# An attention block over 16 images: first image opened in a pinned order, and two inner sums of the third head issued earlier

## The chip, the cores and the metric

The kernel runs on one core of one Trainium2 chip. The metric is device time in microseconds. Five runs of the kernel before lie between 3180.75 and 3183.3, with a median of 3181.74. The profile is one further execution.

In the profile, PE is TensorE's matmul and PEld its weight load, DVE is VectorE, ACT is ScalarE, POOL is GpSimd and SP is SyncE. A letter q behind an engine's name (SPq, ACTq, POOLq) is its sequencer, where transfers are issued. L12 is line 12 of the kernel.

## The reference

For each of 16 images of 512 channels and 32 x 32 = 1024 positions, all in float32:

```python
xg = x.reshape(b, NUM_GROUPS, -1)                       # 8 groups of 64 channels
xn = ((xg - mu) * rsqrt(var + EPS)).reshape(b, c, h, w) * gamma + beta
qkv = einsum('oc,bchw->bohw', qkv_w, xn) + qkv_b        # 1536 x 512
attn = softmax(einsum('bhnd,bhmd->bhnm', q, k) * dh ** -0.5)   # 4 heads of 128
out = einsum('bhnm,bhmd->bhnd', attn, v)
return x + einsum('oc,bchw->bohw', proj_w, out) + proj_b
```

## The kernel before

**Tiles.** An image is four chunks of 128 channels by 1024 positions. Chunks 0 and 1 are the upper rows of the block matrix b (blocks b11 and b12, the left and the right half of the positions), chunks 2 and 3 the lower ones (b21, b22). A float32 matmul shows as two rows in the profile.

**Products by sevens.** The projections for q and k (two pairs of heads), for v and at the end use Strassen's method in Winograd's form: seven products of blocks, with sums of blocks in front and sums of results behind. `FACTORS` names the two factors of each product: 1 is (a11, b11), 2 is (a12, b21), 3 is (s4, b22), 4 is (a22, t4), 5 is (s1, t1), 6 is (s2, t2), 7 is (s3, t3). The weights give s1 = a21 + a22, s2 = s1 - a11, s3 = a11 - a21, s4 = a12 - s2. The images give t1 = b12 - b11, which is written over b12, t2 = b22 - t1, t3 = t2 - b11, t4 = b21 - t2. So b11 and t1 need the upper chunks alone, and t2, t3 and t4 need all. Products go in the `ORDER` 1, 2, 6, 5, 7, 4, 3. `strassen` (L448) holds the accumulation: 1, 6, 7 and 4 share the PSUM bank `x`, 5 and 3 share a bank `y`, and 2 has a `y` bank of its own. The pool has two banks with the tag `y`, and the small products `pm` and `pv` of the group norm use the same tag. The scores use the tag `s` in another pool.

`two_levels` (L514) applies the method twice: four outer groups of at most two products each, and seven inner products in each group. `make_sum` (L526) makes the inner sums t1 to t4 of a group on DVE (L537). For an image's first pair of heads, from image 1 on, they are also kept in DRAM by a transfer on POOL's queue (L541, `sums="keep"`), from where the v products read them. Results of group g are collected in a tile `r` with the tag g % 3, so group 0 of the next products shares its tile with group 3 of the last ones. `v_units` (L680), used for image 0 alone, has one level.

**Image 0.** Its loads are halves of chunks, on the SP and the ACT queue. Constants (gamma, beta and the biases) follow on ACT's queue (L231). `stage_v` and `stage_blocks` put weights on SP's queue. Sixteen matmuls of a constant matrix (`warm`, L1088) keep PE busy while the chunks arrive. `Norm` holds the group norm's steps: `chunk` makes the statistics of a chunk on DVE; `group` averages over channels with a first small matmul (`pm`, L53), makes the variance and averages again (`pv`, L64), then `ve`, a power on POOL (`rstd`, L68) and `sc`; `shift` makes `t` and `sh`; `apply` normalises half a chunk on ACT (L86) or DVE (L89). In image 0 the upper and the lower chunks are two separate groups of statistics. Even chunks are normalised on DVE and odd ones on ACT. For later images ACT makes the statistics from sums and sums of squares (L244 to L250), during the attention of the image ahead.

**Attention.** The main loop runs over heads and eight blocks of 128 keys: scores (L798), exponential on ACT (L804), sum of the exponentials into `tot` on DVE (L810, L812), weighted sum (`po`, L894). `plan_head` deals other work into the eight blocks. During an image's head 1 (the second) these are the projection of the image ahead of it, and the statistics, the normalising and t1 of the next image. During head 2 (the third) it is the q and k products of the next image's first pair. The projection's `finish` adds bias, residual and results to a tile `y` (L778, L781) and stores it with a transfer on POOL's queue (L782).

**What sets the order.** The framework's scheduler takes traced instructions by priority and by the times that its cost model gives, engine by engine; on the chip each engine then runs its list in order. `tc.high_priority(URGENT)` raises the priority of what is traced inside it. `tc.issue_after(ins)` puts what is traced inside behind `ins` on that instruction's engine, in order of issue only. `tc.keep_in_program_order(ins)` puts `ins` behind the last instruction traced on its engine. Before the change only some of DVE's work in image 0 is held by `issue_after`, behind `ve` of the lower rows or behind a normalising.

Of the kernel before, what the change touches and what calls it, by code (L numbers as in the profile page):

```python
# [16 lines left out]
P = 128  # L17
# [13 lines left out]
class Norm:  # L31


    def __init__(self, nc, gn, ps, avg, neghalf, gamma, beta, ncc, n, tag="acc"):
        self.tag = tag
        self.nc, self.gn, self.ps, self.avg, self.neghalf = nc, gn, ps, avg, neghalf
        self.gamma, self.beta, self.ncc, self.n = gamma, beta, ncc, n

    def chunk(self, mv, x, c):
        nc = self.nc  # L40
        st = self.gn.tile([P, self.n // HALF, 6], F32, tag="st", name="st")
        for h in range(self.n // HALF):
            nc.vector.bn_stats(st[:, h, :], x[:, ts(h, HALF)])
        nc.vector.bn_aggr(mv[:, c, :], st.rearrange("p h s -> p (h s)"))

    def group(self, mv, first=0):


        nc, gn, k = self.nc, self.gn, mv.shape[1]
        mean = gn.tile([P, k], F32, tag="mean", name="mean")  # L50
        nc.vector.tensor_copy(mean, mv[:, :, 0])
        pm = self.ps.tile([P, HALF], F32, tag=self.tag, name="pm")
        nc.tensor.matmul(pm[:, :k], self.avg, mean, start=True, stop=True)  # L53

        d = gn.tile([P, k], F32, tag="d", name="d")
        nc.vector.tensor_sub(d, mean, pm[:, :k])
        d2 = gn.tile([P, k], F32, tag="d2", name="d2")
        nc.vector.tensor_mul(d2, d, d)
        v = gn.tile([P, k], F32, tag="vv", name="vv")
        nc.vector.tensor_add(v, d2, mv[:, :, 1])  # L60
        mu = gn.tile([P, k], F32, tag="mu", name="mu")
        nc.vector.tensor_copy(mu, pm[:, :k])
        pv = self.ps.tile([P, HALF], F32, tag=self.tag, name="pv")
        nc.tensor.matmul(pv[:, :k], self.avg, v, start=True, stop=True)  # L64
        ve = gn.tile([P, k], F32, tag="ve", name="ve")
        self.last = nc.vector.tensor_scalar_add(ve, pv[:, :k], EPS)
        rstd = gn.tile([P, k], F32, tag="rstd", name="rstd")
        nc.gpsimd.tensor_tensor(rstd, ve, self.neghalf[:, :k], ALU.pow)  # L68
        sc = gn.tile([P, k], F32, tag="sc", name="sc")
        nc.vector.tensor_mul(sc, rstd, self.gamma[:, first : first + k])  # L70
        return mu, sc

    def shift(self, mu, sc, first=0):

        nc, k = self.nc, mu.shape[1]
        t = self.gn.tile([P, k], F32, tag="t", name="t")
        nc.vector.tensor_mul(t, mu, sc)
        sh = self.gn.tile([P, k], F32, tag="sh", name="sh")
        nc.vector.tensor_sub(sh, self.beta[:, first : first + k], t)
        return sh  # L80
# [76 lines left out]
KC = 2  # L157
# [6 lines left out]
def fast_path(ctx, tc, x, sources, out, consts, flag, dims):  # L164
# [63 lines left out]
    for t, src in (  # L228
        (gamma_sb, gamma), (beta_sb, beta), (qkb_sb, qk_b), (vb_sb, v_b), (projb_sb, proj_b)
    ):  # L230
        nc.scalar.dma_start(t, src)  # L231

    norm = Norm(nc, gn, ps_a, avg, neghalf, gamma_sb, beta_sb, NCC, N, "y")

    def stats_chunk(b, c):
        if c == 0:
            mvs[b] = gn.tile([P, NCC, 2], F32, tag="mv", name=f"mv_{b}")
        if b == 0:
            norm.chunk(mvs[b], xs[b, c], c)
            return  # L240

        junk = lpool.tile([P, N], F32, tag="tt", name=f"junk_{b}_{c}")
        sums = gn.tile([P, 3], F32, tag="st", name=f"sums_{b}_{c}")
        nc.scalar.activation(junk, xs[b, c], AF.Identity, accum_out=sums[:, 0:1])  # L244
        nc.scalar.mul(mvs[b][:, c, 0:1], sums[:, 0:1], 1.0 / N)
        nc.scalar.mul(sums[:, 1:2], sums[:, 0:1], -1.0 / N)
        nc.scalar.activation(
            junk, xs[b, c], AF.Square, bias=sums[:, 1:2], accum_out=sums[:, 2:3]
        )
        nc.scalar.mul(mvs[b][:, c, 1:2], sums[:, 2:3], 1.0 / N)  # L250

    def stats_group(b, first=0, last=NCC):
        mu, sc = norm.group(mvs[b][:, first:last, :], first)
        sh = norm.shift(mu, sc, first)
        for c in range(first, last):
            scaled[b, c] = sc, sh, c - first

    def normalise(b, c, half):
        t = xs[b, c][:, ts(half, HALF)]
        sc, sh, i = scaled[b, c]  # L260

        return norm.apply(t, t, sc, sh, i, b > 0 or c % 2 == 1)

# [156 lines left out]
    def stage_v():  # L420
# [8 lines left out]
        base = 2 * C  # L429
        for n in ("a11", "a12", "a21", "a22"):  # L430
            r, kk = int(n[1]) - 1, int(n[2]) - 1
            for k in range(KC):
                nc.sync.dma_start(
                    wv[n][:, k, :], qkv_wT[ts(KC * kk + k, P), ds(base + r * HC, HC)]
                )

    def v_sums():
        nc.vector.tensor_sub(wv["s3"], wv["a11"], wv["a21"])
        nc.vector.tensor_sub(wv["s4"], wv["a12"], wv["s2"])

# [3 lines left out]
    def run(units):  # L444
        for u in units:
            u()

    def strassen(name, mm, out_, width=HALF):  # L448

# [18 lines left out]
        def p2():  # L468
            t["y"] = bank("y")
            mm(t["y"], 2, True)  # L470
            out_("c11", t["y"], t["p1"])

# [21 lines left out]
        units = {1: p1, 2: p2, 3: p3, 4: p4, 5: p5, 6: p6, 7: p7}  # L494
        return [units[i] for i in ORDER]

    def two_levels(name, site, b, blocks, finish, sums="make", homes="BBBB", prepare=None):
# [31 lines left out]
        def make_sum(g, m):  # L529
# [5 lines left out]
            }[m]  # L535
            for i in range(n):
                nc.vector.tensor_sub(to[:, i, :], inner_block(g, i, a), inner_block(g, i, c))  # L537
            if sums == "keep":
# [137 lines left out]
    def v_units(b, jj):  # L676
# [28 lines left out]

        return strassen(f"v_{b}_{jj}", mm, out_)

# [380 lines left out]
    def warm(n, name):  # L1088

        acc = ps_s.tile([P, HALF], F32, tag="s", name=name)  # L1090
        for _ in range(n):
            ins = nc.tensor.matmul(acc[:, :P], avg, avg, start=True, stop=True)
            tc.keep_in_program_order(ins)

    stage_v()
    stage_blocks(0)
    warm(16, "warm")

    for c in range(KC):
        stats_chunk(0, c)  # L1100
    with tc.high_priority(URGENT):
        stats_group(0, 0, KC)
        for half in range(NH2):
            for c in range(KC):
                upper = normalise(0, c, half)
    for c in range(KC, NCC):
        stats_chunk(0, c)
    stats_group(0, KC, NCC)
    before_power = norm.last
    for half in range(NH2):  # L1110
        for c in range(KC, NCC):
            ins = normalise(0, c, half)
            last_normal = ins if c % 2 == 0 else last_normal
    with tc.issue_after(before_power.ins):
        nc.vector.tensor_add(wv["s1"], wv["a21"], wv["a22"])
        nc.vector.tensor_sub(wv["s2"], wv["s1"], wv["a11"])
        x_sums(0, (1,))
    with tc.issue_after(last_normal.ins):
        sums_of_b(xb[0], (2, 3))
        v_sums()  # L1120
    run(staggered([v_units(0, 0), v_units(0, 1)], (0, 1)))
    stage_sums(0)
    run(staggered(qk_groups(0, 0)))
    next_v, next_qk = [], [qk_groups(0, 1)]
# [168 lines left out]
```

## Time and profile before

| | |
|---|---|
| median of 5 runs | 3181.74 us (3180.75 to 3183.3) |
| the profiled execution | 3181.31 us |
| its span on the core | 3179.5 us |
| PE busy | 3163.6 us, 99% of the span |
| DVE busy | 2630.4 us, 83% |
| ACT busy | 1441.7 us, 45% |
| POOL busy | 514.8 us, 16% |
| matmuls of the scores and of the weighted sum | 1047.1 and 1048.9 us |
| first v matmul of image 0 | at 13.78 us |
| first q and k matmul of image 0 | at 39.91 us |

The span is the time from the first to the last instruction on the core. A group of rows in a timeline gives start, length, engine, line, operation, output and inputs, and the count; in square brackets stands the idle time of the engine ahead of it and what ended that. Matmuls overlap in the pipeline, and their ends are modelled: where a few tenths matter, the starts of successive rows are compared.

### The profile page before, as it was taken

Reading aid. Unit: us, or ns where it says so; the run is one execution under the profiler, and the core shown is the slowest. Engines: PE = TensorE matmul, PEld = TensorE weight load, DVE = VectorE, ACT = ScalarE, POOL = GpSimd, SP = SyncE. Lnnn points to the kernel's source line nnn. Section 1 sums busy time; section 2 is a strip of 40 time slices with the busy share of each in tenths; the row PEclk is TensorE's granted clock in tenths of the full one; section 3 lists DMA queues with packets and bytes.
Section 4 is the critical chain, followed back from the end, with each engine's and each line's share of the span. In section 5 each row is a group of like instructions: output and inputs, shape, how many; then the busy total and the mean of one; then the engine's idle time right before and its main releaser. Section 6 shows DMA issues by size and latency. Waiting matters only on the chain.

```text
span 3179.5 us, 34082 instructions
## 1 busy us (share of the span) xinstructions
PE 3163.6 (99%) x10496; PEld 2187.6 (69%) x10496; DVE 2630.4 (83%) x4634; ACT 1441.7 (45%) x2709; POOL 514.8 (16%) x893
## 2 busy tenths in 40 slices
PE   9999999999999999999999999999999999999999
PEld 7566676676766766677666677667676676766764
DVE  8878979788897888878888787987879978788784
ACT  2535435354353543535435454453534545344342
POOL 0011221111211112211122111222012221122200
PEclk9999999999999999999999999999999999999999
DMA  5655554545545555454554545555455553555531
GB/s 169 214 185 158 183 177 148 176 151 193 166 158 162 163 182 176 163 168 145 191 173 159 175 140 188 167 173 175 138 179 170 176 183 132 181 160 184 181 126 41
DMA packets 211308, 526.92 MB, mean 166 GB/s; under 512 B 32816, under 2 KB 65840, under 8 KB 211120
## 3 DMA queue, kind: packets, MB, share of 16 engines
q1 hardware_dynamic: 133312, 284.74, 28.7%
q0 software_dynamic: 63840, 204.53, 18.9%
q10 hardware_dynamic: 13968, 35.41, 3.5%
q8 instruction: 86, 1.41, 0.2%
q14 instruction: 102, 0.84, 0.1%
HBM read 389.56 MB, written 135.00 MB: 165 GB/s over the span
## 4 chain that ended last, share of the span: by engine, by line
PE 87%; DVE 10%; issue 2%; POOL 1%; DMA 1%; SPq 0%; ACT 0%; ACTq 0%; POOLq 0%; DVEq 0%
PE po L894 24%; PE s L798 24%; PE qk_x L567 12%; PE qk_y L567 9%; PE v_x L567 6%; PE v_y L567 4%; PE pp_x L567 4%; PE pp_y L567 3%; DVE y L781 2%; DVE tot L812 2%; DVE y L778 2%; DVE pp_r L587 1%; DVE pp_r L634 1%; POOL rstd L68 1%; DVE o L904 1%
## 5 line engine op out<-in xcount | busy, mean ns | idle before, releaser
L894 PE MATMUL po<-p,v 128*128 128x512 f32 x2048 | 1048.9, 594 | 0.0
L798 PE MATMUL s<-qk,qk 128*128 128x512 f32 x2048 | 1047.1, 593 | 1.3 <-ACT p L804 1.3
L804 ACT ACTIVATE p<-s 128x512 f32<-128x512 f32 x1024 | 610.6, 597 | 932.8 <-PE s L798 931.6
L894 PEld LDWEIGHTS po<-p,v 128*128 128x128 f32 x2048 | 602.8, 302 | 316.9 <-issue 212.1
L812 DVE TENSOR_TENSOR tot<-tot,p 128x1024 f32<-128x1024 f32 x385 | 470.0, 1221 | 161.6 <-ACT p L804 161.6
L798 PEld LDWEIGHTS s<-qk,qk 128*128 128x128 f32 x2048 | 387.6, 190 | 89.1 <-issue 28.0
L567 PEld LDWEIGHTS qk_x<-qk_t,w 128*128 128x128 f32 x1344 | 250.4, 190 | 171.6 <-issue 76.4
L567 PE MATMUL qk_x<-qk_t,w 128*128 128x256 f32 x1344 | 357.3, 382 | 1.1 <-ACT qk_u L461 1.1
L461 ACT COPY qk_u<-qk_x 128x512 f32<-128x512 f32 (+1 forms) x256 | 136.3, 533 | 230.9 <-PE qk_x L567 226.1
L731 POOL DMA_DIRECT2D vd<-vu x120 | 66.6, 557 | 909.6 <-DVE vu L723 902.3
L587 DVE TENSOR_TENSOR qk_r<-qk_y,qk_u 128x512 f32<-128x512 f32 (+1 forms) x256 | 158.6, 620 | 36.5 <-ACT qk_u L461 22.4
L567 PE MATMUL pp_x<-pp_t,w_proj 128*128 128x256 f32 x630 | 169.3, 385 | 0.0
L782 POOL DMA_DIRECT2D out_y<-y x120 | 66.0, 550 | 632.7 <-DVE y L781 630.5
L587 DVE TENSOR_TENSOR v_r<-v_y,v_u 128x512 f32<-128x512 f32 (+1 forms) x120 | 76.2, 635 | 110.5 <-ACT v_u L461 80.3
L736 POOL DMA_DIRECT2D v<-vd x240 | 140.5, 592 | 162.5 <-DMA vd<-vu 78.5
L567 PE MATMUL v_x<-v_t,w_v 128*128 128x256 f32 x630 | 166.6, 381 | 0.0
L541 POOL DMA_DIRECT2D kept_t<-qk_t x240 | 129.2, 540 | 223.5 <-DVE qk_t L537 204.0
L567 PEld LDWEIGHTS pp_x<-pp_t,w_proj 128*128 128x128 f32 x630 | 116.1, 190 | 64.2 <-issue 22.2
L567 PEld LDWEIGHTS v_x<-v_t,w_v 128*128 128x128 f32 x630 | 118.4, 190 | 55.3 <-issue 19.1
L567 PE MATMUL qk_y<-x,w 128*128 128x256 f32 x512 | 141.8, 379 | 0.0
L666 DVE SCALAR_TENSOR_TENSOR qk<-qk_r,qkb_sb,qk_r 128x512 f32<-128x512 f32 x192 | 137.8, 745 | 1.6
L461 ACT COPY v_u<-v_x 128x512 f32<-128x512 f32 (+1 forms) x124 | 66.3, 535 | 156.8 <-PE v_x L567 130.3
(204 smaller groups left out, 4491.9 us busy)
## 6 DMA issues: line engine op xcount, KB each, us to landing
kept_t<-qk_t POOLq DMA_DIRECT2D x180, 256.0 KB, 3.1
w<-kept SPq DMA_DIRECT2D x90, 512.0 KB, 4.0
v_t<-kept_t SPq DMA_DIRECT2D x180, 256.0 KB, 2.9
w<-kept SPq DMA_DIRECT2D x90, 384.0 KB, 3.4
rinv<-row ACTq DMA_DIRECT2D x63, 512.0 KB, 4.8
x<-in_x POOLq DMA_DIRECT2D x60, 512.0 KB, 5.1
vd<-vu POOLq DMA_DIRECT2D x120, 256.0 KB, 3.0
v<-vd POOLq DMA_DIRECT2D x240, 128.0 KB, 4.2
```

Source lines behind the costliest of these rows:

```text
L461: nc.scalar.copy(t[n][:, :width], t["x"][:, :width])
L541: nc.gpsimd.dma_start(t, to)
L567: nc.tensor.matmul(acc[:, ts(i, Q)], have["w"][t][:, i, slot, :], inner(i, bn), start=(first and i == 0), stop=True, skip_group_check=True,)
L587: nc.vector.tensor_add(dst, view(a), view(c))
L666: nc.vector.scalar_tensor_tensor(st[b, h][:, ts(half, HALF)], a, qkb_sb[:, i : i + 1], c, ALU.add, ALU.add)
L731: nc.gpsimd.dma_start(rows[which][ts(h, P), :], u)
L736: nc.gpsimd.dma_start(vs[b, pair][ts(q, BLK), half].rearrange("m h (k i) j -> m (h k) (i j)", k=n), rows[which].rearrange("(k m) (q e) -> ...
L782: nc.gpsimd.dma_start(out[b, ts(o, P), ts(half, HALF)], t)
L798: nc.tensor.matmul(sc, ks[b, h][:, ts(j, P)], qs[b, h][:, ts(half, HALF)], start=True, stop=True)
L804: exps[s] = nc.scalar.activation(ps[s][:, ts(half, HALF)], sc, AF.Exp, scale=SCALE)
L812: added[b, h, j] = nc.vector.tensor_add(tot[b, h][:, i], tot[b, h][:, i], ps[s][:, i])
L894: nc.tensor.matmul(po[b, h][:, i], v_block(b, h, j), ps[s][:, i], start=(j == 0), stop=(j == NB - 1),)
```

## The change

It has two parts.

The first is `open_image`, which replaces the opening of image 0. Most of its instructions on DVE, and the upper rows' on PE, are pinned to their order in the program. The `Norm` methods are cut into lists of steps for this (`chunk_steps`, `group_steps`), with the same instructions. Twenty warm matmuls stand ahead of `pm`, two between `pm` and `pv`, eight behind `pv`. Chunk 3's statistics are made on ACT. The upper rows' left halves are both normalised on DVE and their right halves on ACT; the lower rows stay as before. v's products are run in the order 1, 5, 2, 6, 7, 4, 3, both units abreast, and product 2 has a bank with the tag `s`. The constants are loaded on POOL's queue. v's weights arrive in the order a11, a21, a22, a12. All DVE work of the v units and of the first pair's q and k products comes behind the last t2.

The second is in `make_sum`: from image 1 on, t1 and t2 of group 0 of the first pair are issued behind the last addition to `tot` of the head ahead, with raised priority.

```diff
-        nc.scalar.dma_start(t, src)
+        nc.gpsimd.dma_start(t, src)
...
-        for n in ("a11", "a12", "a21", "a22"):
+        for n in ("a11", "a21", "a22", "a12"):
...
         def p2():
-            t["y"] = bank("y")
-            mm(t["y"], 2, True)
-            out_("c11", t["y"], t["p1"])
+            own = upper_first
+            acc = ps_s.tile([P, HALF], F32, tag="s", name=f"{name}_z") if own else bank("y")
+            mm(acc, 2, True)
+            out_("c11", acc, t["p1"])
...
-        return [units[i] for i in ORDER]
+        return [units[i] for i in ((1, 5, 2, 6, 7, 4, 3) if upper_first else ORDER)]
...
-            for i in range(n):
-                nc.vector.tensor_sub(to[:, i, :], inner_block(g, i, a), inner_block(g, i, c))
+            with ExitStack() as order:
+                if sums == "keep" and g == 0 and m in ("t1", "t2"):
+                    order.enter_context(tc.issue_after(added[b - 1, 1, NB - 1].ins))
+                    order.enter_context(tc.high_priority(URGENT))
+                for i in range(n):
+                    nc.vector.tensor_sub(
+                        to[:, i, :], inner_block(g, i, a), inner_block(g, i, c)
+                    )
...
+    def open_image():
+        pin = tc.keep_in_program_order
+        norm.pin = pin
...
+        warm(20, "warm_0")
+        for c in range(KC):
+            steps(norm.chunk_steps(mvs[0], xs[0, c], c), 0, 1, 2)
+        with tc.high_priority(URGENT):
+            g = norm.group_steps(mvs[0][:, upper, :])
+            steps(g[:2], 0, 1)
+            warm(2, "warm_1")
+            steps(g[2:8], 0, 1, 2, 3, 4, 5)
+            warm(8, "warm_2")
+
+        stats_chunk(0, NCC - 1)
+        third = norm.chunk_steps(mvs[0], xs[0, KC], KC)
+        steps(third[:1], 0)
+        steps(g[8:], 0, 1)
+        shift(g, upper)
+        for half in range(NH2):
+            for c in range(KC):
+                pin(normalise(0, c, half, half == 1))
+        steps(third[1:], 0, 1)
+        with tc.high_priority(URGENT):
+            g = norm.group_steps(mvs[0][:, lower, :], KC)
+            steps(g[:2], 0)
+            sum_(wv["s1"], wv["a21"], wv["a22"], True)
+            steps(g[2:7], 0, 1, 2, 3)
+        xb[0] = halves([xs[0, c] for c in range(NCC)], "x")
+        bl = xb[0]
+        sum_(bl["t1"][0], bl["b12"][0], bl["b11"][0])
+        with tc.high_priority(URGENT):
+            steps(g[7:9], 0, 1)
+        sum_(bl["t1"][1], bl["b12"][1], bl["b11"][1])
+        with tc.high_priority(URGENT):
+            steps(g[9:], 0)
+        shift(g, lower)
+        for half in range(NH2):
+            for c in range(KC, NCC):
+                pin(normalise(0, c, half, c % 2 == 1))
+        norm.pin = lambda ins: ins
+        sum_(wv["s2"], wv["s1"], wv["a11"])
+        for k in range(KC):
+            last = sum_(bl["t2"][k], bl["b22"][k], bl["t1"][k])
+        with tc.issue_after(last.ins):
+            for k in range(KC):
+                nc.vector.tensor_sub(bl["t3"][k], bl["t2"][k], bl["b11"][k])
+            nc.vector.tensor_sub(wv["s3"], wv["a11"], wv["a21"])
+            for k in range(KC):
+                nc.vector.tensor_sub(bl["t4"][k], bl["b21"][k], bl["t2"][k])
+            nc.vector.tensor_sub(wv["s4"], wv["a12"], wv["s2"])
+        return last
...
-    warm(16, "warm")
...
-    run(staggered([v_units(0, 0), v_units(0, 1)], (0, 1)))
-    stage_sums(0)
-    run(staggered(qk_groups(0, 0)))
+    opened = open_image()
+    with tc.issue_after(opened.ins):
+        run(staggered([v_units(0, 0), v_units(0, 1)], (0, 0)))
+        stage_sums(0)
+        run(staggered(qk_groups(0, 0)))
```

## The prediction

> **What bounds the kernel now.** First the page's table of busy times and PE's own waits.
>
> ```profile
> PE 3163.6 (99%) x10496; PEld 2187.6 (69%) x10496; DVE 2630.4 (83%) x4634; ACT 1441.7 (45%) x2709; POOL 514.8 (16%) x893
> ...
> PE pv L64 <- DVE vv L60: 2.5, 2, 1.3
> PE qk_y L567 <- DVE qk_t L537: 2.2, 14, 0.2
> PE warm L1092 <- DVE avg L225: 1.5, 1, 1.5
> PE pm L53 <- DVE mean L51: 1.3, 1, 1.3
> ```
>
> PE is the bound: a change can win only where PE waits or runs slowly. The waits of any size are in the opening (warm, pm, pv), plus one small wait that comes back 14 times. The clock column of the stretches shows what waits alone don't (columns: busy us of PE, PEld, DVE, ACT, POOL, then the granted clock):
>
> ```profile
> 9.00:10.00 1.00, 0.38 (x2) 0.30 (x2) 1.00 (x5) 0.00 (x0) 0.00 (x0) 1.00 0.48 134
> 10.00:11.00 1.00, 0.03 (x1) 0.04 (x1) 1.00 (x6) 0.00 (x0) 0.00 (x0) 0.87 0.74 169
> 16.00:17.00 1.00, 1.00 (x4) 0.75 (x3) 1.00 (x5) 0.00 (x0) 0.00 (x0) 0.50 0.72 194
> 18.00:19.00 1.00, 1.00 (x7) 0.87 (x6) 1.00 (x4) 1.00 (x3) 0.00 (x0) 1.00 0.90 266
> 20.00:60.00 40.00, 40.00 (x184) 34.03 (x184) 38.81 (x92) 10.91 (x20) 0.00 (x0) 1.00 0.43 143
> ```
>
> The clock falls to 0.50 after PE had little to do, and v's first products pay for it. The last line matters later: DVE is nearly full behind a full PE. Third, the timeline of the opening:
>
> ```profile
> 7.63 0.69 DVE L43 BATCH_NORM_STATS2 st<-x 128x6 f32<-128x512 f32 x1 [0.60 <-DMA x<-in_x]
> 9.39 0.38 PE L53 MATMUL pm<-mean,avg 128*128 128x2 f32 x2 [1.30 <-DVE mean L51]
> 10.97 0.59 PE L64 MATMUL pv<-vv,avg 128*128 128x2 f32 x2 [1.20 <-DVE vv L60]
> 13.78 5.57 PE L684 MATMUL v_x<-wv_a,x 128*128 128x256 f32 x16
> 31.27 3.62 PE L684 MATMUL v_x<-wv_a,xt 128*128 128x256 f32 x16
> ```
>
> The first 16 v matmuls take 5.57 us, sixteen of the same kind 3.62 once the clock is full. Last, the start of a third head (image 5's; the others look alike):
>
> ```profile
> 1128.16 1.22 DVE L812 TENSOR_TENSOR tot<-tot,p 128x1024 f32<-128x1024 f32 x1
> 1129.29 0.69 DVE L781 TENSOR_TENSOR y<-y,pp_r 128x512 f32<-128x512 f32 x1
> 1129.89 0.75 DVE L778 SCALAR_TENSOR_TENSOR y<-pp_r,projb_sb,y 128x512 f32<-128x512 f32 x1
> 1130.56 0.43 DVE L537 TENSOR_TENSOR qk_t<-x 128x256 f32<-128x256 f32 x1
> 1130.89 0.69 DVE L781 TENSOR_TENSOR y<-y,pp_r 128x512 f32<-128x512 f32 x1
> 1131.22 0.59 PE L567 MATMUL qk_y<-qk_t,w 128*128 128x256 f32 x2
> 1131.49 0.43 DVE L537 TENSOR_TENSOR qk_t<-x 128x256 f32<-128x256 f32 x1
> 1131.98 0.70 PE L567 MATMUL qk_y<-qk_t,w 128*128 128x256 f32 x2 [0.16 <-DVE qk_t L537]
> 1132.51 1.02 PE L798 MATMUL s<-qk,qk 128*128 128x512 f32 x2
> ```
>
> The second t1 sum waits behind the projection's last additions, and PE waits for it. The row says 0.16 because ends are modelled; read the starts. A row of this form occupies PE for 0.216 (sixteen in 3.62, of which the last shows 0.38), a pair for 0.43. Here the next start comes 0.76 after the first pair and 0.53 after the second: 0.33 and 0.10, together 0.43 lost.
>
> **Third head's first sums.** Four inner sums of group 0 (t1 and t2, two each) go directly behind `tot`'s eighth addition. Nothing is added, but DVE's order changes: they start at 0.33 spacing (1130.56 to 1130.89) from 1129.3, and the last is done by 1130.7, ahead of the wait at 1131.65. Their inputs are there: the outer t1 (L283) ends by 1127.9. Gain 14 x 0.43 = 6.0 us. The trace's fifteenth third head (image 0) starts on another wait, so I count 14; 15 would be 6.5. What moves back is y's three additions, by 4 x 0.33 = 1.3 us. They feed only POOL's output DMAs, with nothing on PE behind them. Behind them stands qk's first c11 addition (1131.83), which writes the result tile that the projection's last group still occupies: 0.7 us later (1129.3 + 1.3 + 1.97 for the three = 1132.57). It releases a `y` bank; next taken by qk at 1141.20, 8.7 us on. t2's DMA to the kept sums goes out on POOL earlier, before the last output DMAs instead of after (1131.88, 1132.41); each is 0.54 of a POOL busy 16%.
>
> **The opening up to v.** DVE's aggregate of chunk 1 stood behind a chunk 2 half that waited 0.60 for its transfer; pinned in order, the mean is ready by 7.4. But PE now runs 20 warm matmuls first: sixteen (32 rows) took 6.60, four more take 0.9 at full rate (0.113 a row, half of 3.62/16) or 1.65 at the average. pm thus starts at 8.9 to 9.7 against 9.39; I take 8.9, as the tail is the fast part. From there by rows: pm to d 0.45, three small DVE steps 0.17 each, pv to ve 0.62, ve to the power 0.25, power to sc 0.75, sc to the first normalise 0.59, that to the first v matmul 0.60: 12.6 instead of 13.78. Gain 1.2 (0.3 at the other end). The warm matmuls between pm, pv and v (2 and 8) fill gaps of 1.30 and 1.20 (0.45 and 1.8 us at 0.113 a row), leaving about 0.4 and 0.6. With that I expect the clock to hold: 5.57 - 3.62 = 1.95 more. The other end is nothing, if it falls again.
> [...]
>
> **The lower rows inside v.** The second pm and pv now run between v's products: 133.09 to 133.34 and 135.27 to 135.51 in a later image, so 0.5 us. The new product order (1, 5, 2, ...) puts lower rows third. By 3.62 a pair of products, v 1 starts at 12.6, 5 at 16.7, 2 at 20.3, 6 at 23.9, 7 at 27.5. DVE, in pinned order: two normalises to 13.0, statistics 0.64 + 0.19, mean, s1 0.68 while pm runs, four small steps to 15.2, t1 0.69, ve, t1 by 16.6, power 1.08, sc and shift to 17.6, normalise to 18.7, s2 and t2 to 20.6, t3, s3, t4, s4 to 24.5. Only t1 is close (16.6 against a second step at 17.1). ACT takes chunk 3's statistics: 1.05 + 1.14 and four reads and scalings of 0.19 from the landing at 9.3 (its bn_stats started 9.24) gives 12.5, then 2 x 0.8 to 14.1, in front of t1. Bounds 0 to 1.5 lost here.
>
> **Costed at nothing.** Constants go from ACT's queue to POOL's: five of 0.55 each from 0.8, landing within 5.1 (the x rows of POOL), so by 8.7, when gamma is wanted at 11.5. If that cover went, sc would wait and v with it, microsecond for microsecond.
> [...]
> v's weights in order a11, a21, a22, a12 are the same eight transfers. p2's own bank comes from the scores' pair, free until 65. DVE behind the opening: s4 ends at 24.5 instead of 23.34 while PE is 2.65 ahead, so DVE is 3.8 us tighter. Cover: qk's third group of weights ends at 41.35 (L413 at 40.93) and its first product runs at 50.64; the first group's has over 10 us. If it is not enough, up to 2.65 goes.
>
> **Sum.** 6.0 + 1.2 + 1.95 - 0.5 = 8.65. The profiled execution took 3181.31 (span 3179.5): 3172.7. The median 3181.74 stands 0.43 higher: 3173.1.
>
> **Rivals.** 0.2% is 6.4 us, about what a measurement here can tell from no change.
> A, the opening gives nothing (clock falls again, or PE waits at t1, pm or for DVE's backlog): 3181.7 - 6.0 = 3175.7, up to 3177 with a microsecond of new waits. For it: DVE's 38.81 of 40. Against: the slack above.
> B, the change doesn't do what it says: the third head's sums do not help, because another addition is late in their place (the c11 addition, t3 at 1133.1): 3181.7 - 2.65 = 3179.1. Against: DVE's total in that stretch is unchanged, and p6 at 1133.37 and what follows had its sums in time.
> C, slower: the c11 addition, 0.7 late, holds the bank or result tile that PE's next group wants, in 15 images: 15 x 0.74 = 11.1 - 2.65 gives 3190.2. It decides from 0.19 us an image (2.65/15), by more than the measure from 0.6. Against: 8.7 us of slack on the bank. An order made anew by the planner could shrink it.
> D, better: fifteen heads at 0.43, pm as soon as the mean is there (7.4, another 1.5), small matmuls hidden: 3170.5 or less.
>
> **How the numbers follow.** Forecast (3170.5 to 3175.3) 0.60, A 0.15, B 0.09, C 0.09, D 0.07. Faster: forecast and D, 0.67. Same: A and B, 0.24. Slower: C, 0.09. The range leaves out C and the far part of D: 3169.5 to 3179.5; the forecast's own is 3170.5 to 3175.3.
>
> **What would show it.** Right: no line of PE qk_y waiting for qk_t 14 times; pairs of qk_y starting 0.43 apart; four L537 rows in a row behind L812; granted clock 1.00 from 10 on; v's first 16 rows in about 3.6 from 12.6; qk's first product near 37.2 instead of 39.91. Wrong: a clock of 0.50 in 10 to 18, v_x waiting for wv_s or x sums, or a new PE wait repeated by image.

## The result, and the profile after

The changed kernel takes 3174.48 us (median of 25 runs, 3173.08 to 3176.53) against 3181.68 us (45 runs, 3179.92 to 3183.3). The ratio is 0.9978, with a 95% interval of 0.9973 to 0.9984: 7.2 us less. The interval lies clear of 1, but it reaches across 0.998, so the change is faster by about the 0.2% that the prediction took as what can be told from no change. The profiled execution took 3174.56 us, its span is 3172.8 us.

The total is near the forecast of 3173.1, but not for the reasons given. The third heads brought more than forecast, and the opening brought almost nothing to the end. The page's busy times first.

```profile
PE 3159.3 (100%) x10524; PEld 2197.8 (69%) x10524; DVE 2629.7 (83%) x4631; ACT 1443.4 (45%) x2716; POOL 515.6 (16%) x898
```

PE is busy for 4.3 us less (3163.6 before), although it runs 28 rows more, the warm matmuls. Busy time counts a slow clock and modelled ends too, so it is not a count of work. PE's own waits in the changed kernel (total us, times, longest) are more telling:

```profile
PE qk_x L592 <- ACT qk_r L610: 1.9, 1, 1.9
PE warm L1117 <- DVE avg L248: 1.5, 1, 1.5
...
PE pm L83 <- DVE mean L82: 1.2, 1, 1.2
PE qk_x L592 <- DMA w<-kept: 0.8, 1, 0.8
```

The wait of `qk_y` for `qk_t`, 14 times, is gone, and so are the waits for `vv` (2.5) and the early `pm` (1.3). Two large ones are new: 1.9 at a q and k product, and 1.2 at `pm`. Both lie in image 0, the second at the statistics of image 1. The granted clock (the column behind POOL's) over the same stretches as before:

```profile
9.00:10.00 1.00, 0.91 (x9) 0.72 (x8) 0.53 (x5) 0.55 (x1) 0.00 (x0) 1.00 1.05 323
10.00:11.00 1.00, 1.00 (x12) 1.00 (x11) 0.76 (x3) 0.94 (x5) 0.72 (x1) 1.00 0.83 261
...
16.00:17.00 1.00, 1.00 (x7) 0.87 (x6) 0.38 (x3) 0.58 (x1) 0.71 (x1) 1.00 0.99 287
...
20.00:60.00 40.00, 39.59 (x179) 32.92 (x177) 39.91 (x93) 11.46 (x21) 0.00 (x0) 1.00 0.43 140
```

The clock stays at 1.00. The last row says the rest: PE, which had no idle time in these 40 us, now has some, and DVE is busy for 39.91 of 40 where it was 38.81. The opening on PE:

```profile
8.52 0.28 PE L83 MATMUL pm<-mean,avg 128*128 128x2 f32 x2
...
9.44 0.39 PE L88 MATMUL pv<-vv,avg 128*128 128x2 f32 x2
9.68 2.03 PE L1117 MATMUL warm<-avg 128*128 128x128 f32 x16
12.05 1.99 PE L709 MATMUL v_x<-wv_a,x 128*128 128x256 f32 x8 [0.34 <-DVE x L112]
13.88 0.28 PE L83 MATMUL pm<-mean,avg 128*128 128x2 f32 x2
14.02 1.11 PE L709 MATMUL v_x<-wv_a,x 128*128 128x256 f32 x4
...
16.07 3.62 PE L709 MATMUL v_y<-wv_s,x 128*128 128x256 f32 x16
```

v begins at 12.05 instead of 13.78. Its first 16 rows, with `pm` and `pv` between them, go from 12.05 to 16.07, and the first q and k product starts at 36.79 instead of 39.91. Image 5's third head:

```profile
1126.33 1.22 DVE L837 TENSOR_TENSOR tot<-tot,p 128x1024 f32<-128x1024 f32 x1
...
1127.46 0.76 DVE L560 TENSOR_TENSOR qk_t<-x 128x256 f32<-128x256 f32 x2
...
1128.13 0.76 DVE L560 TENSOR_TENSOR qk_t<-x,qk_t 128x256 f32<-128x256 f32 x2
...
1128.80 0.69 DVE L806 TENSOR_TENSOR y<-y,pp_r 128x512 f32<-128x512 f32 x1
...
1129.39 1.03 PE L592 MATMUL qk_x<-qk_t,w 128*128 128x256 f32 x4
...
1130.25 1.03 PE L592 MATMUL qk_y<-qk_t,w 128*128 128x256 f32 x4
...
1131.11 1.02 PE L823 MATMUL s<-qk,qk 128*128 128x512 f32 x2
...
1131.34 0.69 DVE L612 TENSOR_TENSOR qk_r<-qk_y,qk_p 128x512 f32<-128x512 f32 x1
```

The four inner sums stand directly behind `tot`, the projection's additions behind them, and four rows of PE take 0.86: two pairs at 0.43, with nothing between. The scheduler changed PE's order here as well: product 6 (`qk_x`, with t2) now runs ahead of product 5 (`qk_y`, with t1) and of the scores, where before it ran behind them, at 1133.37. That order alone could not have helped the kernel before, whose t2 sums (1132.43) came later than product 5 started (1131.22). Whether the earlier sums would do as well under PE's old order was not tried.

To see where the time went, take the start of the same matmul of the scores in both traces and subtract. This "lead" of the changed kernel on the profiled execution of before is 3.12 us at the first q and k product, 1.49 at the ninth row of the scores (at 73 us), -0.30 at the first scores of image 1 (at 243 us), and then grows by 0.40 to 0.67 in each of 14 images, to 7.0. In image 5, for example, it is 1.84 up to the third head and 2.35 behind it. So the opening's 3.12 is gone by the end of image 0, and the 14 third heads earned 7.3. The experiments ask for the cause of both.

### The profile page after: what moved, and what is told of

It is laid out like the page before. It is cut to its first block, busy times and chain, and to the rows that moved or that the text cites. A ratio compares the mean times of both kernels' runs of the same rounds, so it can differ in the third digit from the quotient of the medians.

```text
span 3172.8 us, 34154 instructions
## 1 busy us (share of the span) xinstructions
PE 3159.3 (100%) x10524; PEld 2197.8 (69%) x10524; DVE 2629.7 (83%) x4631; ACT 1443.4 (45%) x2716; POOL 515.6 (16%) x898
## 3 DMA queue, kind: packets, MB, share of 16 engines
q8 instruction: 87, 1.43, 0.2%
## 4 chain that ended last, share of the span: by engine, by line
PE 96%; DVE 2%; DMA 1%; issue 0%; SPq 0%; ACTq 0%; POOL 0%; ACT 0%; DVEq 0%
PE po L919 27%; PE s L823 27%; PE qk_x L592 12%; PE qk_y L592 9%; PE pp_x L592 6%; PE v_x L592 6%; PE v_y L592 4%; PE pp_y L592 4%; PE lx L1003 0%; DVE qk_t L560 0%; DMA x<-in_x 0%; PE ly L1003 0%; DMA w<-kept 0%; DMA st_a<-in_proj_wT 0%; DVE qk_r L612 0%
## 5 line engine op out<-in xcount | busy, mean ns | idle before, releaser
L691 DVE SCALAR_TENSOR_TENSOR qk<-qk_r,qkb_sb,qk_r 128x512 f32<-128x512 f32 x192 | 137.8, 745 | 1.6
```

Source lines behind the costliest of these rows:

```text
L691: nc.vector.scalar_tensor_tensor(st[b, h][:, ts(half, HALF)], a, qkb_sb[:, i : i + 1], c, ALU.add, ALU.add)
```

## The experiments

The lead is given at the first q and k product (Q), the ninth row of the scores (S), the first scores of image 1 (I1) and of image 15 (I15), each against the same profiled execution of before. It is exact for one pair of executions, while the medians carry the spread of the runs: the changed kernel gains 7.2 us by the medians in one measurement and 5.9 in another. So a difference of less than about a microsecond between two medians decides nothing here, and the readings rest on the starts. The profiled execution need not be a typical one either: of the first hold, again, and of the changed kernel, again, it was the fastest of its runs, and of the opening only one of the two slowest. No kernel here leaves out any part of the computation; in the one without fillers, ten constant matmuls that no result depends on are missing.

| kernel | v starts | lead at Q | S | I1 | I15 | median, and that of before beside it |
|---|---|---|---|---|---|---|
| changed | 12.05 | 3.12 | 1.49 | -0.30 | 7.00 | 3174.48 / 3181.68 |
| sums only | 12.98 | 0.42 | 0.42 | -0.32 | 6.32 | 3175.04 / 3181.98 |
| opening only | 11.49 | 3.68 | 0.36 | -0.25 | -0.24 | 3181.82 / 3181.98 |
| later start | 12.84 | 2.44 | 0.91 | 0.08 | 6.08 | 3175.76 / 3181.98 |
| no fillers | 11.52 | -0.06 | -0.07 | -1.53 | 5.67 | 3175.6 / 3181.41 |
| first hold | 12.39 | 2.77 | 2.33 | 1.20 | 7.97 | 3174.05 / 3181.98 |
| first hold, again | 11.42 | 3.75 | 3.31 | 1.73 | 8.65 | 3173.5 / 3181.11 |
| changed, again | 11.42 | 3.75 | 2.04 | 0.73 | 8.11 | 3175.24 / 3181.11 |
| old opening, hold | 13.48 | 0.78 | 0.77 | 0.19 | 6.37 | 3174.94 / 3181.41 |
| long hold | 11.37 | 3.79 | 2.17 | -3.17 | 4.00 | 3176.93 / 3181.41 |
| both holds | 12.11 | 3.06 | 2.63 | -0.74 | 5.70 | 3175.24 / 3181.41 |
| first hold and the short one | 11.76 | 3.41 | 2.97 | 0.50 | 7.90 | 3173.84 / 3181.11 |

**The third heads alone.** The kernel before, with nothing but the part in `make_sum`:

```diff
             for i in range(n):
-                nc.vector.tensor_sub(to[:, i, :], inner_block(g, i, a), inner_block(g, i, c))
+            with ExitStack() as order:
+                if sums == "keep" and g == 0 and m in ("t1", "t2"):
+                    order.enter_context(tc.issue_after(added[b - 1, 1, NB - 1].ins))
+                    order.enter_context(tc.high_priority(URGENT))
+                for i in range(n):
+                    nc.vector.tensor_sub(
+                        to[:, i, :], inner_block(g, i, a), inner_block(g, i, c)
+                    )
```

> The kernel before with the third head's first sums alone. Theory A (the opening's lead is lost again inside image 0, and the sums alone carry the gain): from the first scores of image 1 to those of image 15 the gain should grow by about 0.52 us an image, as it does in the changed kernel (from -0.30 to 7.00 over 14 images), and the time is 3174.4, within 1 us of the changed kernel's 3174.48. Rival B (the terms of the prediction: sums worth 6.0, opening part of the rest): 3175.7.

Measured: 3175.04 us (3173.76 to 3176.3, 11 runs), ratio 0.9978 (0.9969 to 0.9987), 6.9 us under before. Its lead grows by 6.6 over the 14 images. Nearly the whole result is this part. The other kernels that have it, in the table, gain 6.0 to 7.4 over these images, about 0.5 in most of them, so the prediction's 6.0 was somewhat low.

**The opening alone.** The changed kernel without that part:

```diff
-            with ExitStack() as order:
-                if sums == "keep" and g == 0 and m in ("t1", "t2"):
-                    order.enter_context(tc.issue_after(added[b - 1, 1, NB - 1].ins))
-                    order.enter_context(tc.high_priority(URGENT))
-                for i in range(n):
...
+            for i in range(n):
+                nc.vector.tensor_sub(to[:, i, :], inner_block(g, i, a), inner_block(g, i, c))
```

> The changed kernel without the third head's part. Theory A: 3181.7 to 3182, no gain, although v starts at 12.05 and q and k at 36.8 as in the changed kernel; the lead of 3.1 us there is gone by the third head of image 0. Rival B: 3179.1 by the prediction's 2.65, or 3180.5 where half of it is kept.

Measured: 3181.82 us (3179.73 to 3183.53), ratio 0.9999 (0.999 to 1.0008). By the medians the opening is worth 0.16 us at the end, though it reaches the first q and k product 3.68 us earlier. The interval of the ratio, nearly 3 us wide each way, would by itself leave room for the 2.65 of the prediction; the lead does not, for 3.3 of it is gone by 74 us and it is -0.25 at I1. Three of the eleven runs (3179.73, 3180.22 and 3180.45) are under the fastest of before (3180.62), so some executions may keep a part; the record has no profile of these. The profiled one took 3183.36: it lost 1.7 more in image 15, behind I15, where PE once waits 1.43 for DVE. The largest loss is near 60 us. PE's products there:

```profile
59.08 0.59 PE L584 MATMUL qk_x<-x,w 128*128 128x256 f32 x2
61.54 0.70 PE L584 MATMUL qk_x<-x,w 128*128 128x256 f32 x2 [1.86 <-ACT qk_r L602]
...
62.93 2.73 PE L584 MATMUL qk_y<-x,w 128*128 128x256 f32 x6
```

The rows start 2.46 apart where a pair takes 0.43: a stall of 2.03. The six rows from 62.93 then take 2.5 us instead of 1.3, because the granted clock fell to 0.50 behind the stall:

```profile
62.00:63.00 1.00, 1.00 (x5) 0.50 (x4) 1.00 (x4) 0.00 (x0) 0.00 (x0) 0.98 0.91 356
63.00:64.00 1.00, 1.00 (x4) 0.81 (x3) 0.74 (x3) 0.60 (x1) 0.00 (x0) 0.50 0.04 16
...
65.00:66.00 1.00, 1.00 (x3) 0.67 (x2) 1.00 (x3) 0.00 (x0) 0.00 (x0) 0.50 0.46 131
66.00:67.00 1.00, 1.00 (x4) 0.43 (x3) 1.00 (x4) 0.00 (x0) 0.00 (x0) 0.81 0.00 0
```

**Is the lead absorbed by something at a fixed time?** The changed kernel with 16 warm matmuls instead of 8 in front of v:

```diff
-            warm(8, "warm_2")
+            warm(16, "warm_2")
```

> The changed kernel with 16 warm matmuls instead of 8 between pv and v, so that v starts about 1.2 us later (8 more at 0.215 less the 0.5 of idle time there now). Theory A (the lead is absorbed by waits at fixed times in image 0): the time stays within 0.5 us of 3174.5, and the wait of pm near 132.8 shrinks by what the start lost. Rival B (a lead in the opening goes through to the end): 3175.7.

Measured: 3175.76 us (3174.64 to 3176.72), ratio 0.9979 (0.997 to 0.9988). v starts 0.8 later than in the changed kernel's profile and the first q and k product 0.7 later. Up to S this delay stays (0.58 of it), and the stall moves with the start: it stands at 62.67, and is 2.03 again. A fixed time, such as a transfer that PE catches up with, would have swallowed the delay there. So this stall is made by the order of the work, not by a point in time. Behind it theory A fares better: the wait at `pm` falls from 1.2 to 0.4, as it said, and at I1 the late start is not behind (0.08 against -0.30). That its median gain is 6.2 instead of 7.2, near rival B's number, does not come from the delay: its lead is 0.9 smaller at I15 because it grows by 6.0 behind I1 instead of 7.3, and why is open.

**What the stall waits for.** The same place in the changed kernel, in its timeline of PE, of ACT, of DVE and of SP's queue:

```profile
59.21 0.60 PE L592 MATMUL qk_y<-qk_t,w 128*128 128x256 f32 x2
59.64 0.59 PE L592 MATMUL qk_x<-x,w 128*128 128x256 f32 x2
62.11 0.69 PE L592 MATMUL qk_x<-x,w 128*128 128x256 f32 x2 [1.87 <-ACT qk_r L610]
...
61.67 0.37 ACT L610 COPY qk_r<-qk_x 128x256 f32<-128x256 f32 x1 [0.81 <-DVE qk L691]
...
58.42 0.41 DVE L411 TENSOR_TENSOR w<-st 128x256 f32<-128x256 f32 x1
...
59.89 0.42 DVE L411 TENSOR_TENSOR w<-st 128x256 f32<-128x256 f32 x1
60.23 1.41 DVE L691 SCALAR_TENSOR_TENSOR qk<-qk_r,qkb_sb,qk_r 128x512 f32<-128x512 f32 x2
...
64.54 0.41 DVE L429 TENSOR_TENSOR w<-w 128x256 f32<-128x256 f32 x1
...
59.84 4.65 SPq L402 DMA_DIRECT2D w<-in_qkv_wT  x2
```

Two conditions end together. ACT's copy that empties the bank (61.67 to 62.04) waits for a result tile that DVE's L691 still reads. And the raw block of weights for this product is loaded into a tile that comes free when the products at 59.21 end: issued at 59.84, it lands 2.1 us later (the median of issue to landing in that stretch), at 61.97. In the second run of the changed kernel the same stall, 2.14 long, is put down to the transfer:

```profile
61.57 0.67 PE L592 MATMUL qk_x<-x,w 128*128 128x256 f32 x2 [1.98 <-DMA w<-in_qkv_wT]
```

There ACT's copy ended at 61.40 and the transfer landed at 61.43. By these ends either condition alone would hold PE for about the same time. PE's list has nothing else there: the other products need the second pair's derived weights (L411, L429 and on), and DVE, full and with less time in hand against PE than before, comes to L411 and L429 to L431 at 58.4 to 66.9. In the kernel before, the same sums (there L392 and L410 to L412) are done from 52.9 to 62.3, and PE has only its two short stalls:

```profile
62.29 1.56 PE L567 MATMUL qk_x<-qk_t,w 128*128 128x256 f32 x6 [0.46 <-ACT qk_u L461]
64.53 0.70 PE L567 MATMUL qk_x<-qk_t,w 128*128 128x256 f32 x2 [0.68 <-ACT qk_u L461]
...
52.86 0.42 DVE L392 TENSOR_TENSOR w<-st 128x256 f32<-128x256 f32 x1
...
59.50 0.42 DVE L410 TENSOR_TENSOR w<-w 128x256 f32<-128x256 f32 x1
...
61.91 0.42 DVE L412 TENSOR_TENSOR w<-w 128x256 f32<-128x256 f32 x1
```

**The first hold.** If that is so, an order in which DVE makes the derived weights first should give PE work. The changed kernel, with the two sums of the second pair's staged blocks (`stage_sums(1)`, L374 and L375, needed only by a later group) put behind the last addition of the first pair:

```diff
+    made = {}
...
-            nc.vector.scalar_tensor_tensor(
+            made[b, pair] = nc.vector.scalar_tensor_tensor(
...
-    stage_sums(1)
+    with tc.issue_after(made[0, 0].ins):
+        stage_sums(1)
```

> The changed kernel with the two staging sums for the second pair's weights held behind the first pair's last q and k addition, which takes 1.4 us (and one weight sum of 0.4 behind them) out of DVE's queue ahead of PE's 2.0 us wait at 62.1. Theory A: that wait shrinks to about 0.6, the lead at the first scores grows by 1.4, and the time stays within 0.5 us of 3174.5, since pm waits for the projection's weights at 132.8 whatever the lead. Rival B: 3173.1.

Measured: 3174.05 us (3172.22 to 3174.75, 7 runs), ratio 0.9973 (0.9962 to 0.9984). The lead at S is 2.33 out of 2.77: 0.44 lost instead of 1.63, as theory A says of the wait. The kernel was run again beside the changed kernel, on one chip.

> The changed kernel with the first hold alone, beside the changed kernel itself on one chip. Theory B (the opening's lead is lost in DVE's queue near 62 and a part of it can be had): 0.5 to 1.5 under the changed kernel in this call, lead at the second image 0.8 to 1.5 against the kernel before. Rival (the earlier difference of 0.4 to 0.7 was chance of the transfers near 130 to 156): equal within 0.3.

> The changed kernel itself, as the mate of the two others. If the wait of 1.2 at pm near 132.8 was a chance of when the projection's weights landed, it is 0.2 to 0.6 here and the lead at the second image 0 to 0.8 instead of -0.30; if it belongs to the order of the kernel, it is 1.0 to 1.4 again. The wait of 2.0 near 62 is there in either case.

Measured: with the hold 3173.5 us (3172.7 to 3174.92, 10 runs), ratio 0.9977 (0.9967 to 0.9986); changed kernel 3175.24 us (3173.14 to 3177.55, 11 runs), ratio 0.998 (0.9971 to 0.9989). The intervals of the ratios overlap, but the medians differ by 1.7, in the same direction as in the first measurement (gains of 7.9 and 7.2), and the profiles show the place. Both start v at 11.42 and lead by 3.75 at Q. At S 3.31 are left with the hold and 2.04 without. In place of the 2.14 stall there are two of 0.84, about as before the change (0.63 and 0.84), since the derived weights (L429 and on) now stand in front of 60 and PE has their products to run. PE and DVE of the kernel with the hold:

```profile
59.44 1.10 PE L592 MATMUL qk_x<-qk_t,w 128*128 128x256 f32 x4 [0.68 <-DVE w L431]
61.22 0.70 PE L592 MATMUL qk_x<-qk_t,w 128*128 128x256 f32 x2 [0.68 <-ACT qk_u L477]
...
56.48 0.41 DVE L429 TENSOR_TENSOR w<-w 128x256 f32<-128x256 f32 x1
...
58.89 0.41 DVE L431 TENSOR_TENSOR w<-w 128x256 f32<-128x256 f32 x1
```

The rival, that the difference was chance, expected equality within 0.3, and falls for this stretch: the loss between Q and S is 0.43 or 0.44 in the four profiles with this hold and the new opening, and 1.5 to 1.7 in the four that have the changed kernel's order and kept the clock (later start, changed twice, and the long hold alone, below). Of the 1.3 us that the hold has in hand at S in these two profiles, 1.0 is left at I1 and 0.5 at I15.

**The hold without the opening.** The kernel before with the third heads' sums and the same hold, which together are the two diffs above.

> The old opening with the third head's sums moved and, beside that, the second pair's weight sums held behind the first pair's last addition. Theory B (the 2-us wait near 62 belongs to the new opening, where PE is 3 us earlier against a DVE that is full): the old opening has only its two waits of 0.7 and 1.0 near 62 to 65 to lose, the hold gains 0 to 0.8, lead at the second image at most +0.5, time 3174.3 to 3175.2, and what the hold gained in the changed kernel (0.4 by the medians, 1.2 us of lead at the second image) shows that the opening is worth about that much when DVE lets it through. Theory H (the hold is worth the same anywhere): lead at the second image goes from -0.32 by 1.2 to +0.9, time 3173.8 or less.

Measured: 3174.94 us (3173.82 to 3175.75), ratio 0.9979 (0.997 to 0.9988); against the sums alone 6.5 under its before instead of 6.9. The hold is worth nothing in the old opening, where the lead at S (0.77) is that at Q (0.78) in any case. Where the scheduler made no order with the long stall there is nothing for it to win, and theory B's numbers hold.

**Are the fillers what holds the clock?** The changed kernel without the warm matmuls between `pm` and `pv` and in front of v:

```diff
-            warm(2, "warm_1")
...
-            warm(8, "warm_2")
```

> The changed kernel without the 2 warm matmuls between pm and pv and the 8 between pv and v (no computed value depends on them). Theory W (the prediction's clock term, 1.95 us: the clock holds only because PE is kept at work in these gaps): v starts at the same place (about 12), the granted clock falls to 0.50 within 9 to 18 as it did before the change (rows 0.87 and 0.50 from 10 to 17), v's first 16 rows take about 5.5 us instead of 3.6, the first qk product starts 1.5 to 2 us later (38.3 to 38.8 instead of 36.8). Of that, as in the run with a later start (a delay of 0.7 at the first qk product cost 1.3 at the end), 1 to 2 reach the end: 3175.5 to 3176.5. Theory G (the gaps are short enough by themselves, and the earlier mean already removed the cause of the fall): clock 1.00 throughout, first qk product at 36.8 within 0.3, the time that of the changed kernel within 0.7: 3173.8 to 3175.2.

Measured: 3175.6 us (3172.87 to 3177.55), ratio 0.9981 (0.9972 to 0.999). The opening answers clearly. The last row of `pv` and the first of v start 2.48 us apart, and the clock is at 0.50 from 12.4 to 19.2:

```profile
11.52 1.30 PE L709 MATMUL v_x<-wv_a,x 128*128 128x256 f32 x4 [2.23 <-DVE x L112]
...
12.00:13.00 1.00, 0.82 (x4) 0.28 (x2) 0.86 (x3) 0.97 (x4) 0.00 (x0) 0.70 0.84 260
13.00:14.00 1.00, 0.90 (x3) 0.90 (x4) 0.93 (x4) 1.00 (x3) 0.00 (x0) 0.50 0.78 203
...
18.00:19.00 1.00, 1.00 (x4) 0.82 (x3) 1.00 (x2) 0.47 (x1) 0.00 (x0) 0.50 0.95 274
```

From v's start to the first q and k product it takes 28.44 us; the changed kernel takes 24.74. The lead of 3.12 is wholly gone (-0.06): the fillers are worth 3.7 us in this order, more than the 1.95 that the prediction gave them. Theory W is right about the clock, and at Q too low about its size. At the end its range holds (3175.6, or 5.8 under the kernel before beside it), though the changed kernel's second measurement gained no more (5.9), so that only the leads tell the two apart (5.67 at I15 against 7.00 and 8.11). It holds, but not by its reckoning: the order that the scheduler made here has the two stalls of old (0.63 and 0.84) and loses nothing between Q and S. What the fillers save by 19 us, the stall at 62 takes back for nearly half.

**The rest of image 0.** From S to I1 every kernel loses against the profile of before. In the changed kernel the new `pm` wait stands there. Its `mean`, at 132.54, is queued on DVE behind an addition of the projection's staged weights that waited for their transfer:

```profile
129.53 0.69 DVE L374 TENSOR_TENSOR st_s<-st_a,st_a 128x512 f32<-128x512 f32 x1 [3.62 <-DMA st_a<-in_proj_wT]
```

Three kernels put these sums later: behind image 1's `ve` (in the changed kernel, and with the first hold), and only behind the `mean` (with the first hold).

```diff
-        for step in self.group_steps(mv, first):
-            step()
+        made = [step() for step in self.group_steps(mv, first)]
+        self.ve = made[7]
...
-        if g == 0:
-            stage_sums(site)
-        group_weights(site, g, True)
+        with ExitStack() as order:
+            if site == "proj":
+                order.enter_context(tc.issue_after(norm.ve.ins))
+            if g == 0:
+                stage_sums(site)
+            group_weights(site, g, True)
```

In the third kernel `made[0]` stands for `made[7]`.

> The changed kernel with the projection's weight sums of image 0 held, in program order, until image 1's `ve` (second step of its normalisation statistics) has been issued, so that the mean of image 1 does not stand in DVE's queue behind an addition that waits 3.6 us for the projection's weights. Theory Q (the wait of 1.2 at pm near 132.8 is DVE's order): the pm wait falls to the 0.2 of the kernel before, the lead at the second image's first scores row goes from -0.30 to about +0.8, and the end moves by 1.0: 3173.4 (3172.8 to 3174.0). Theory M (the stretch from 118 to 156 is held by the transfers of the weights themselves, granted DMA share 0.8 there, and the wait only moves): the wait goes on to the w<-kept row near 156 (0.99 now, then about 2), lead at the second image unchanged within 0.4, time 3174.1 to 3174.9.

> The changed kernel with both holds: the second pair's weight sums behind the first pair's last addition, and the projection's weight sums behind image 1's `ve`. Theory Q (both losses are orders of DVE): the gains add, lead of 2.3 at the 48th scores row kept through image 0 up to about 2.0 at the second image, time 3172.2 (3171.5 to 3172.9). Theory M (the transfers hold the later stretch): the first hold's gain alone, lead at the second image 1.2 as in the run with the first hold only, time 3173.7 to 3174.4.

> The changed kernel with the second pair's weight sums held behind the first pair's last addition and, beside that, the projection's first weight sums held only behind image 1's mean, not behind the later `ve`: they start about 1.8 us later than with the first hold alone, instead of 5.8 later as with the long hold. Theory Q (the pm wait is DVE's order, and what the long hold lost was its length): no pm wait (0.4 before), no new waits of 2 us at the scores, lead at the second image 1.2 to 1.8, time 0.0 to 0.7 under that with the first hold alone in the same call. Theory M (that stretch is held by the transfers): the wait for the kept weights near 155 grows from 1.25 by what the pm wait loses, lead at the second image 1.2 or less, time equal within 0.3 or above.

Measured: the long hold 3176.93 us (3176.35 to 3177.74), ratio 0.9985 (0.9976 to 0.9994); both holds 3175.24 us (3174.61 to 3176.74), ratio 0.998 (0.9971 to 0.9989); first hold and the short one 3173.84 us (3172.89 to 3177.0), ratio 0.9978 (0.9969 to 0.9987). In all three the `pm` wait is gone, as theory Q says, and in none of them is there a gain: with the long hold and with both, the times lie above the ranges of both theories. With the long hold PE waits twice for the exponentials, because the weight sums now stand in front of `tot`, whose tiles the exponentials need. The wait of the long hold alone, and below it PE with the short hold:

```profile
PE s L823 <- ACT p L829: 3.8, 2, 2.0
```

```profile
156.65 2.04 PE L592 MATMUL qk_x<-x,w 128*128 128x256 f32 x4 [2.69 <-DMA w<-kept]
158.48 1.62 PE L592 MATMUL qk_y<-x,w 128*128 128x256 f32 x4
```

With the short hold the wait goes to the load of the kept weights (2.69 where the first hold has 1.1 to 1.3), and the first four rows behind it take 1.83 instead of 0.86, 2.1 times as long: by an estimate from these starts, a clock of 0.50. So the `pm` wait is an order of DVE, but the stretch as a whole is not freed by changing that order, as theory M says. What of the loss between S and I1 belongs to the change stays open. The two kernels with the old opening and the sums lose 0.58 and 0.74 there too, and the opening alone 0.61; the changed kernel, the later start, the first hold and the kernel without fillers lose 0.8 to 1.8, and the wait at `pm` alone varies with the landing of the weights (from start to start 1.37 too much in the first profile of the changed kernel, 0.82 in the second).

## Why the prediction was right or wrong

**The total** (3173.1 forecast, 3174.48 measured) came out near by luck: two errors of opposite sign met. The third heads gave 7.3 in the profiled execution instead of 6.0, and the opening's 2.65 was gone by I1 (-0.30). In the medians the sums alone are at 6.9, the opening alone at 0.16 and both together at 7.2. Rival A's 3175.7 was as near to the measured time as the forecast: 1.2 off against 1.4.

**Third heads: right in mechanism, 0.43 an image too low.** The wait is gone, the pairs are 0.43 apart, the four sums stand behind `tot`, and there are 14 of them. The lead grows by 0.52 an image on the mean. 0.43 of it is the two gaps that were read; 0.07 comes from a later `qk_x` wait that also fell away, and two images give a little more. The first `c11` addition was said to be 0.7 later. It is: it stands 5.01 behind `tot`'s start instead of 3.67, 1.34 later, and no wait follows from it in any image. Rival C had the right step and no price (its limit, 2.65/15, is 0.18 and not 0.19), and rival B (another addition late in place of the sums) falls with the run of the sums alone.

**v's start: right, mis-sized by little.** 12.05 against 12.6 forecast, 11.4 to 12.4 over the profiles with 8 fillers. The opening also varies from run to run with the same order. The starts of the warm rows are 0.213 us apart at first and 0.112 afterwards, and in the changed kernel's profile this turns near 6.7 us, in that of before near 7.3. With the new opening v starts the later, the later these rows are done: `pm`, the next in PE's list, starts at 7.83 to 7.86 in the four profiles where v starts at 11.37 to 11.49, at 8.22 where v starts at 11.76 and at 8.52 where it starts at 12.05. The old one started v at 13.78, 12.98 and 13.48 in three profiles, so that the profile of before was the latest of them. On the mean the first q and k product moved from 39.5 (the three with the old opening) to 36.5 (the eight with the new one and 8 fillers), 3.0 us.

**Lower rows inside v: right.** From v's start to the first q and k product the changed kernel takes 24.74. Before it was 26.13, of which 1.95 was the slow clock, so 24.18: 0.56 more, forecast 0.5. The first 16 rows of v, with the two small matmuls between them, show 0.40 of it (4.02 from start to start instead of 3.62). Neither t1 nor ACT's chunk 3 nor the constants on POOL's queue held anything: the list of PE's waits has no row for them.

**Clock: right that it holds, and by the cause given.** It is 1.00 in all rows of the opening, and without the fillers it is not. At Q the forecast of 2.65 met 3.12. The clock fell behind a gap of 2.48 without the fillers, and behind one of 2.03 in the kernel with the opening alone. The last section has such gaps beside the clock that was read behind them.

**Where it failed: "Costed at nothing", DVE behind the opening.** The step said that DVE ends s4 at 24.5 while PE is 2.65 ahead, 3.8 us tighter, and named as cover the third group's weights (41.35, used at 50.64). The last sum, s4, ended at 23.75, and the cover named did hold: nothing waits there. What was not looked at is the work behind it. DVE was at 38.81 of 40 and went to 39.91. Here the full engine did not make up its lag but handed it on to the next place where PE has no slack, the change of pairs at 56 to 65 us, where the kernel before already stood for 0.63 and 0.84. Moreover the scheduler remade the order there: in both kernels the staged sums stand ahead of the derived weights, but these came some 5 us later than before (58.4 to 66.9 instead of 52.9 to 62.3), and PE was left with one product whose weights were still on the way. Why it did so is not shown. The first hold, which undoes this order, takes back about 1.2 of the 1.63 us lost between Q and S. The other 1.79, lost between S and I1, are open in part: 0.6 to 0.7 of them are lost by the kernels with one part of the change too, and the `pm` wait took 1.37 in this execution, though the kernels without that wait were not faster. The step's own last sentence, "up to 2.65 goes", named the price. So rival A's mechanism ("DVE's backlog"), with 15 in 100 given to it, is near what happened to the opening, more by the order of DVE's queue than by its length, while its total of 3175.7 missed by what the third heads gave more.

## What to carry to other kernels

A lead won ahead of a stretch in which another engine is 97% busy has to be followed through that stretch, to the next place where the fast engine already waits: compare the starts of the same instruction in both traces all along, and not the waits at the point that was changed. A reordering that a scheduler works out again can spoil a place that the diff doesn't touch, so look at what each engine runs in the next 50 us and pin the one or two instructions that must not come first; here holding two additions back saved 1.2 us up to the scores, of which some was lost again later. Small gains that come back in each of many images (0.5 us, 14 times) outlast larger ones that are had once.

## What the runs showed of the hardware

The clock's fall is not a matter of the gap's length alone. The table has PE's idle time as the profile gives it, ahead of the row that starts at the time named, and the granted clock that the rows of the stretches show behind it (its ends worked out from the rows that hold them):

| profile | PE idle, us | ahead of the row at, us | clock behind it |
|---|---|---|---|
| before | 1.30 and 1.20 | 9.39 and 10.97 | 0.50 from 10.7 to 17.6 |
| no fillers | 2.23 | 11.52 | 0.50 from 12.4 to 19.2 |
| opening only | 1.86 | 61.54 | 0.50 from 63.0 to 66.4 |
| long hold | 2.03, the sum from 150 to 158 | | 0.50 from 158.8 to 165.7 |
| changed | 1.87 | 62.11 | 1.00 from 60 to 66 |
| later start | 1.86 | 62.67 | 1.00 from 61 to 65 |
| changed, again | 1.98 | 61.57 | 1.00 from 62 to 66 |
| both holds | 2.03 | 157.38 | 1.00 from 157 to 162 |

At nearly the same place the clock fell behind 1.86 us with the opening alone and stayed at 1.00 behind 1.86, 1.87 and 1.98 in three other profiles; before the change it fell with gaps of 1.30 and 1.20. What decides between them is not shown, and no run varied the idle time on purpose.

Where the clock fell, it cost beside the stall 1.6 us in the kernel with the opening alone (3.3 lost between Q and S instead of 1.7), and 3.7 in the opening without fillers.
